# Extra matmuls of ones, an earlier first mask, and values weighed before scores in a twelve-sublayer decoder

## The chip, the core and the metric

The kernel runs on one core of one Trainium2 chip. The metric is the device time of one execution in microseconds (us). A core has five engines with instruction queues of their own: TensorE (PE in the profile; PEld is its weight load), VectorE (DVE), ScalarE (ACT), GpSimd (POOL) and SyncE (SP, which issues DMAs). Each takes its own instructions in order, and semaphores connect them.

## The reference

A batch of 16 sequences of 64 tokens with 128 features passes through four decoder layers. Each of the twelve sublayers is followed by a residual sum and a layer normalization. What is computed, cut to the calls:

```python
x = _layernorm(x + linear_attention(x))                 # 16 heads of 8
x = _layernorm(x + cross_attention(ctx, x, ctx, mask))  # xa0: 16 heads
x = _layernorm(x + local_block(x))                      # lb: two layers of local attention and a gated MLP
x = _layernorm(x + self_attention(x))                   # at1
x = _layernorm(x + cross_attention(x, ctx, ctx))        # xa1
x = _layernorm(x + sorted_ffn(x))                       # sf: only half 0 has work
x = _layernorm(x + recurrence(x))                       # rc: relu(mix), decaying scan, projection
x = _layernorm(x + cross_attention(x, ctx, ctx, mask))  # xa2: 32 heads
x = _layernorm(x + switch_ffn(x))                       # sw: 16 experts, top 1
x = _layernorm(x + relative_attention(x))               # at3
x = _layernorm(x + cross_attention(x, ctx, ctx, mask))  # xa3
x = _layernorm(x + top2_ffn(x))                         # tt: 8 experts, top 2
```

Linear attention normalizes queries and keys to unit length, forms `A = k^T (v * w)` for each token position over the batch, and gives `q A`. The local block normalizes queries and keys, turns them by position, and takes a softmax over the tokens of a window of 64, before and after which half of the features are shifted by one token.

## The kernel before

**Layout.** The 1024 tokens are two halves of 512 (8 sequences each). Activations lie token by token (`xt`, 128 tokens by 4 by 128 features) and flipped (`x`, features by 512 tokens). PSUM is shared out as two buffers of two banks for scores (pool `psc`, tag `sc`) and four buffers of one bank for everything else (pool `pt`, tag `t`). A tile waits until an earlier user of its buffer has been read.

**The order of the work.** The kernel is written as Python generators, one for each half; `side_by_side` takes a step of each in turn, with half 0 five steps ahead in the first stream (xa0, lb, at1, xa1, sf, rc, xa2). The framework's scheduler then sets the order in which each engine's queue holds the instructions, so an added instruction can move others. At sw both halves meet; a second stream (at3, xa3) and tt follow.

**`keep_busy`** (L153) issues one matmul of a bf16 tile of ones with itself, 512 columns wide. Its result is overwritten by the next real matmul into the same PSUM tile; it exists only to give TensorE something to do.

**Linear attention** (L266) works in four pairs of groups of 128 rows. `front` projects into `la_ps`, squares, and gets inverse roots (L764). `back` multiplies the three parts of `la_ps` by their factors (L314, DVE) into `la_four`, spreads values on POOL (L321, `la_sq`), multiplies keys by values (L327, `la_a`), masks on DVE (L329, `la_am`), transposes the queries (L333, into `la_o`), applies `la_am` (L339), and flips back (L346, L348, L351). `la_ps` and `la_o` share the four `t` buffers.

**Attention** (`attention`, L408): keys are copied under a mask for each head (L441, POOL, `km`), a unit of scores is made (L480) with its mask added by a matmul (L491), DVE takes maximum and difference (L536, L537), ACT the exponential (L540), `turn` transposes (L551, L554), `weigh` multiplies by the values (L572), and `gather` flips the result. Masks are made at their first use; xa0's `mask_outer` (L698) has two DMAs on SP (L704), a POOL multiply (L709, `mo_m`) and a DVE conversion to bf16 (L710, `mo_b`).

**The local block** (`local_half`, L784) runs its two units u through `rotate` (L807 to L840, `lb_qk`), `flip` (L862 to L869), `weights` (L880 to L905: scores `lb_sc`, maximum, difference, exponential), `turn` (L914), `weigh` (L932 to L949, `lb_av`, `lb_ao`), `gather` (L957, `lb_pao`) and `put` (L968), then the MLP (L1043 to L1063, `lb_pg`, `lb_pa`, `lb_pw`).

**The end of a sublayer** (`close`, L185): statistics on DVE (L195, L197), the inverse deviation on POOL (L201, L204, `rstd`), the normalized tokens on DVE (L206, `xt`), and then in `flip` an optional number `ones` of `keep_busy` matmuls, four transposes into `px` (L224, or L235 with the shift) and a copy by ACT (L226).

**The recurrence** (L1115) mixes neighbours on DVE (L1127, L1128), projects (`rc_p`, L1132), takes a ReLU on ACT (L1134), scans on DVE (L1137), and projects back (`po_rc`, L1142).

Of the kernel before, what the change touches and what calls it, by code (L numbers as in the profile page):

```python
# [37 lines left out]
class Kernel:  # L38
# [227 lines left out]
    def linear_attention(self):  # L266


        nc, work, psc, pt = self.nc, self.aw, self.psc, self.pt
        att = self.buf(4, [N], "la_att")  # L270
        att_b = att.rearrange("p (s b j) -> p s b j", b=S // 2, j=2)
        blk8 = self.g("blk8").unsqueeze(1).to_broadcast([P, 8, P])
        pos4 = self.g("pos4").unsqueeze(2).to_broadcast([P, 4, P])

        def front(pair):
            ss = work.tile([P, 2, 32], F32, tag="la_ss", name=f"la_ss{pair}")
            made = []
            for i in range(2):
                gr = pair * 2 + i
                ps = self.psum(pt, f"la_ps{gr}")  # L280

                for _ in range(12 if gr == 0 else 1):
                    self.keep_busy(ps)
                w = self.g("L0a_w")
                n = w.shape[1]
                nc.tensor.matmul(
                    ps[:, :n], self.x_all[:, bass.ts(gr, P)], w, start=True, stop=False
                )

                rows = [self.la_b] if pair == 0 else la_b3  # L290
                ones = self.g("one") if pair == 0 else self.ones_b
                for row in rows:
                    nc.tensor.matmul(
                        ps[:, :n], ones[0:1, :], row, start=False, stop=row is rows[-1]
                    )
                sq = self.buf(2, [HALF], f"la_sq{gr}")
                nc.scalar.activation(sq[:, 0:256], ps[:, 0:256], AF.Square)
                nc.vector.tensor_reduce(
                    ss[:, i, :], sq[:, 0:256].rearrange("p (n d) -> p n d", d=8), AX.X, ALU.add
                )  # L300
                gates = work.tile([P, 32], F32, tag="la_g", name=f"la_g{gr}", bufs=4)
                nc.scalar.activation(gates, ps[:, 384:416], AF.Sigmoid)
                made.append((ps, sq, gates))
            return made, self.inverse_root(work, ss.rearrange("p i n -> p (i n)"), f"la_{pair}")

        def back(pair, made, rs):
            for i, (ps, sq, gates) in enumerate(made):
                gr = pair * 2 + i
                four = self.buf(2, [4, P], f"la_four{gr}")
                rq = work.tile([P, 16], F32, tag="la_rq", name=f"la_rq{gr}")  # L310
                nc.vector.tensor_tensor(rq, rs[:, i * 32 : i * 32 + 16], gates[:, 16:32], ALU.mult)
                factors = (rq, rs[:, i * 32 + 16 : i * 32 + 32], gates[:, 0:16])
                for n, by in enumerate(factors):
                    nc.vector.tensor_tensor(  # L314
                        four[:, n, :].rearrange("p (h d) -> p h d", d=8),
                        ps[:, bass.ts(n, P)].rearrange("p (h d) -> p h d", d=8),
                        by.unsqueeze(2).to_broadcast([P, 16, 8]),
                        ALU.mult,
                    )
                vm = sq.rearrange("p (i d) -> p i d", d=P)  # L320
                nc.gpsimd.tensor_tensor(  # L321
                    vm, four[:, 2, :].unsqueeze(1).to_broadcast([P, 4, P]), pos4, ALU.mult
                )
                a = psc.tile([P, 2, HALF], F32, tag="sc", name=f"la_a{gr}")
                for t in range(2):
                    r = slice(64 * t, 64 * t + 64)
                    nc.tensor.matmul(a[:, t, :], four[r, 1, :], sq[r, :], start=True, stop=True)  # L327
                am = self.buf(4, [8, P], f"la_am{gr}")
                nc.vector.tensor_tensor(  # L329
                    am, a.rearrange("p t (i d) -> p (t i) d", d=P), blk8, ALU.mult  # L330
                )
                po = pt.tile([P, 4, P], F32, tag="t", name=f"la_o{gr}")
                nc.tensor.transpose(po[:, 0, :], four[:, 0, :], self.g("ident"))  # L333
                nc.scalar.copy(four[:, 3, :], po[:, 0, :])

                for m in range(2):
                    for j in range(4):
                        at = (m * 4 + j) // 2 * 32
                        nc.tensor.matmul(  # L339
                            po[32 * j : 32 * j + 32, 1 + m, :],  # L340
                            four[:, 3, at : at + 32],
                            am[:, m * 4 + j, :],
                            start=True,
                            stop=True,
                        )
                nc.scalar.copy(four[:, 0:2, :], po[:, 1:3, :])  # L346
                for m in range(2):
                    nc.tensor.transpose(po[:, 1 + m, :], four[:, m, :], self.g("ident"))  # L348
                to = po[:, 1:3, :].rearrange("p m (a b) -> p m a b", b=64)
                for j in range(2):  # L350
                    nc.scalar.copy(  # L351
                        att_b[:, :, gr * 4 : gr * 4 + 4, j].rearrange("p s (m a) -> p m a s", m=2),
                        to[:, :, :, 48 * j : 48 * j + 16],
                    )
        fronts = [front(0)]
        la_b3 = []
        rows3 = self.lbp.tile([P, 2080], F32, tag="v0", name="la_b3").bitcast(BF16)
        for i in range(3):
            row = rows3[0:1, bass.ts(i, 416)]
            nc.vector.tensor_copy(row, self.la_b)  # L360
            if i < 2:
                nc.vector.tensor_tensor(self.la_b, self.la_b, row, ALU.subtract)
            la_b3.append(row)
        for pair in range(4):
            if pair < 3:
                fronts.append(front(pair + 1))
            back(pair, *fronts[pair])
        return self.project_close(pt, self.g("L0a_wo"), att, "L0a_bo", "la")


# [37 lines left out]
    def attention(  # L408
        self, h, tag, kv, hd, scale, wq, wk, wv, wo, bq=None, bk=None, bv=None, bo=None,
# [4 lines left out]
        work, psc, pt = self.aw, self.psc, self.pt  # L414
# [104 lines left out]
        y = self.new_y(tag, h) if wo is None else None  # L519
# [101 lines left out]
        if wo is not None:  # L621
            for u in list(aos):
                gather(u)
            ps = pt.tile([P, 4, D], F32, tag="t", name=f"po_{tag}{h}")
            for i in range(4):
                self.group(ps[:, i, :], [(att[:, bass.ts(i, P)], self.g(wo))])
            y = self.new_y(tag, h)
# [6 lines left out]
            else:  # L634
                nc.vector.tensor_tensor(y, ps, base, ALU.add)

        ones = 8 if h == 1 and tag in ("xa2", "xa3") else 1
        flip = self.close(pt, h, y, tag, shift=tag == "xa0", ones=ones)
        yield "last"
        flip()  # L640
# [143 lines left out]
    def local_half(self, h):  # L784

        nc = self.nc
        work, psc, pt = self.aw, self.psc, self.pt
# [3 lines left out]
        for l in range(2):  # L791
            tag = f"lb{l}{h}"
# [195 lines left out]
            turn(0)  # L988
            flip(1)
            yield  # L990
            weights(1)
            weigh(0)
            yield
            turn(1)
            gather(0, 1)
# [24 lines left out]
            ps = self.psum(pt, f"{tag}_phn")  # L1020
# [31 lines left out]
            ps = pt.tile([P, 4, D], F32, tag="t", name=f"{tag}_pw2")  # L1052
# [8 lines left out]
            if l == 0:  # L1061
                x_in = self.buf(2, [4, D], f"{tag}_x2")
                nc.vector.tensor_tensor(x_in, ps, base, ALU.add)  # L1063
                self.shifted(self.psum(pt, f"{tag}_px"), h, x_in)
                yield
            else:
                y = self.new_y("lb", h)
                nc.vector.tensor_tensor(y, ps, base, ALU.add)
                flip = self.close(pt, h, y, "lb")
                yield "last"  # L1070
                flip()

# [2 lines left out]
    def sorted_ffn(self, h):  # L1075
        nc, pt = self.nc, self.pt
        yield
        x = self.x[h]
        if h == 1:
            flip = self.close(pt, h, self.xt[h], "sf")  # L1080
# [10 lines left out]
        for c in range(8):  # L1091
            if c % 4 == 0:
                hids.append(self.buf(8, [4, HALF], f"sf_hid{c}"))
            ps = self.psum(pt, f"sf_p{c}")
# [10 lines left out]
        y = self.new_y("sf", h)  # L1105
        for i in range(4):
            nc.vector.scalar_tensor_tensor(
                y[:, i, :], acc[:, i, :], ws[:, i : i + 1], self.xt[h][:, i, :], ALU.mult, ALU.add
            )
        flip = self.close(pt, h, y, "sf")  # L1110
        yield "last"
        flip()

# [1 line left out]
    def recurrence(self, h):  # L1115
        nc, pt, sc = self.nc, self.pt, self.scalars
# [12 lines left out]
            inp[:, :, 1:S], x3[:, :, 0 : S - 1], rest, inp[:, :, 1:S], ALU.mult, ALU.add  # L1129
        )  # L1130
        ps = self.psum(pt, f"rc_p{h}")
        self.group(ps, [(self.g("rc_win"), inp.rearrange("p b s -> p (b s)"))])  # L1132
        hid = self.buf(2, [HALF], f"rc_hid{h}")
        nc.scalar.activation(hid, ps, AF.Relu, bias=self.g("rc_bin"))  # L1134
# [3 lines left out]
            st, dec.rearrange("p b s -> p (b s)"), hid, 0.0, ALU.mult, ALU.add  # L1138
        )
        ps = pt.tile([P, 4, D], F32, tag="t", name=f"po_rc{h}")  # L1140
        for i in range(4):
            self.group(ps[:, i, :], [(st[:, bass.ts(i, P)], self.g("rc_wout"))])  # L1142
        y = self.new_y("rc", h)
        nc.vector.tensor_tensor(y, ps, base, ALU.add)
        flip = self.close(pt, h, y, "rc")
        yield "last"
        flip()

# [863 lines left out]
```

## Time and profile before

| what | us |
|---|---|
| median of 3 runs | 896.4 (886.66 to 896.52) |
| the profiled execution | 871.75 |
| its span, first to last instruction | 869.8 |
| TensorE busy | 717.0 (82%) |
| VectorE busy | 481.7 (55%) |
| ScalarE busy | 354.9 (41%) |
| GpSimd busy | 254.0 (29%) |
| mean granted TensorE clock | 0.893 of full speed |

The profile is one execution. Busy time is time in which an engine had an instruction running. PEclk is the clock that TensorE was granted, in tenths of full speed. A row of the timeline gives start, duration, engine, source line, operation, the tiles written and read, shapes and a count, and in brackets how long the engine was idle before it and which instruction ended that. An f32 matmul leaves two records for each instruction, so "x8" is four matmuls.

### The profile page before, as it was taken

To read this page: it belongs to the slowest core of one execution; us is meant where nothing else is said; L and a number is where in the kernel's file an instruction comes from. 1 tells how busy PE (TensorE), PEld (TensorE's weight loads), DVE (VectorE), ACT (ScalarE), POOL (GpSimd) and SP (SyncE) were. 2 spreads that over 40 slices of the span, in tenths; PEclk is the share of its full clock that TensorE was granted. 3 is DMA by queue.
4 is the path that set the end of the run, shared out by engine and by line. 5 is a ranking of instruction groups with operands and counts; after the bars stand their busy time and mean duration, and the time that the engine had idled before them with its cause. 6 is when DMAs were issued, how large, how long until landed. Compare 5 with 4: busy or idle time off the path is not lost.

```text
span 869.8 us, 17379 instructions
## 1 busy us (share of the span) xinstructions
PE 717.0 (82%) x7045; PEld 455.8 (52%) x7045; DVE 481.7 (55%) x1103; ACT 354.9 (41%) x584; POOL 254.0 (29%) x289
## 2 busy tenths in 40 slices
PE   6777979878888699789996999977947999967990
PEld 2333646555545466546573557644633565744770
DVE  4556466574665745447525766544542565656563
ACT  2223547445454444445551445522304554522330
POOL 2314135070432703130305220016151111025732
PEclk7878989889999998989996989988977799978995
DMA  7900000000000000140000000051115625031102
GB/s 277 273 1 25 2 1 2 14 1 2 1 2 1 1 2 2 40 155 2 2 2 0 1 2 2 2 151 48 50 41 148 198 54 184 2 122 37 53 25 83
DMA packets 34504, 43.65 MB, mean 50 GB/s; under 512 B 7524, under 2 KB 26469, under 8 KB 33784
## 3 DMA queue, kind: packets, MB, share of 16 engines
q1 hardware_dynamic: 32344, 38.26, 14.1%
q0 software_dynamic: 2080, 4.26, 1.7%
q8 instruction: 58, 0.95, 0.5%
q14 instruction: 22, 0.18, 0.1%
HBM read 34.31 MB, written 11.61 MB: 53 GB/s over the span
## 4 chain that ended last, share of the span: by engine, by line
PE 51%; DVE 18%; POOL 9%; issue 6%; ACT 4%; DMA 4%; SPq 1%; DVEq 0%; POOLq 0%; ACTq 0%
PE xa_sc L480 5%; PE xa_av L572 4%; PE xa_pt L551 3%; PE sw_pe L151 2%; PE at_sc L480 2%; PE lb_qk L151 2%; DVE lb_t L818 2%; PE at_av L572 2%; PE xa_sc L491 2%; DMA at_mem<-at_rsb 2%; DVE lb_t L832 2%; PE xa_pt L156 2%; PE at_pt L551 1%; PE lb_pf L868 1%; PE lb_pw L151 1%
## 5 line engine op out<-in xcount | busy, mean ns | idle before, releaser
L536 DVE TENSOR_REDUCE xa_mx<-xa_sc 128x16 f32<-128x1024 f32 x40 | 48.7, 1218 | 63.8 <-PE xa_sc L491 41.4
L838 POOL TENSOR_TENSOR lb_t<-lb_t,lb_t 128x1024 f32<-128x1024 f32 x16 | 37.7, 2357 | 99.4 <-DVE lb_t L832 95.2
L554 ACT COPY xa_eT<-xa_pt 128x512 f32<-128x512 f32 x80 | 45.5, 587 | 40.8 <-PE xa_pt L551 40.0
L540 ACT ACTIVATE xa_e<-xa_e 128x1024 f32<-128x1024 f32 x40 | 42.3, 1058 | 37.2 <-DVE xa_e L537 37.1
L480 PE MATMUL xa_sc<-xa_km,xa_q 32*64 32x256 f32 x640 | 55.2, 404 | 0.7 <-ACT xa_q L431 0.5
L551 PE MATMUL xa_pt<-const,xa_e 128*128 128x128 f32 x320 | 48.8, 280 | 1.8 <-ACT xa_e L540 1.8
L441 POOL TENSOR_SCALAR xa_km<-xa_k,const 128x512 f32<-128x512 f32 x40 | 27.1, 695 | 79.3 <-ACT xa_k L429 46.0
L537 DVE TENSOR_TENSOR xa_e<-xa_sc,xa_mx 128x1024 f32<-128x1024 f32 x40 | 48.7, 1217 | 2.1
L551 PEld LDWEIGHTS xa_pt<-const,xa_e 128*128 128x128 f32 x320 | 40.3, 145 | 13.1 <-ACT xa_e L540 3.7
L572 PEld LDWEIGHTS xa_av<-v,xa_eT 128*64 128x64 f32 x1280 | 40.5, 138 | 8.2 <-issue 6.1
L572 PE MATMUL xa_av<-v,xa_eT 128*64 128x18 f32 (+1 forms) x1280 | 44.2, 209 | 0.0
L156 PEld LDWEIGHTS <-ones_b 128*128 128x128 bf16 x255 | 24.8, 104 | 36.4 <-issue 19.9
L151 PE MATMUL lb_qk<-w,lb_hs 128*128 128x512 f32 x64 | 35.8, 686 | 8.5 <-DVE lb_t L832 4.8
L480 PEld LDWEIGHTS xa_sc<-xa_km,xa_q 32*64 32x64 f32 x640 | 24.7, 136 | 19.9 <-issue 12.8
L814 DVE TENSOR_REDUCE lb_ss<-lb_t 128x16 f32<-128x1024 f32 x16 | 19.5, 1217 | 27.9 <-ACT lb_t L811 27.9
L201 POOL TENSOR_TENSOR rstd_xa<-mv_xa,eps 128x4 f32<-128x4 f32 x8 | 1.6, 201 | 112.2 <-DVE mv_xa L197 112.2
L156 PE MATMUL xa_pt<-ones_b 128*128 128x512 bf16 x80 | 30.2, 390 | 0.0
L862 POOL TENSOR_TENSOR lb_t<-lb_t,lb_rs 128x1024 f32<-128x1024 f32 x16 | 30.1, 1904 | 0.0
L868 PE MATMUL lb_pf<-const,lb_t 128*128 128x128 f32 x128 | 20.1, 312 | 9.4 <-POOL lb_t L862 9.3
L480 PE MATMUL at_sc<-at_km,at_q 32*64 32x256 f32 x256 | 22.5, 452 | 5.2 <-DVE at_rel L533 3.7
L533 DVE TENSOR_TENSOR at_rel<-at_rel,at_sc 128x1024 f32<-128x1024 f32 x8 | 9.7, 1212 | 29.2 <-DMA at_mem<-at_rsb 16.4
L554 ACT COPY at_eT<-at_pt 128x512 f32<-128x512 f32 x32 | 17.6, 586 | 19.3 <-PE at_pt L551 13.4
(474 smaller groups left out, 1715.0 us busy)
## 6 DMA issues: line engine op xcount, KB each, us to landing
sw_gu<-in_sw_gu SPq DMA_DIRECT2D x4, 1024.0 KB, 8.3
at_mem<-at_rsb SPq DMA_DIRECT2D x16, 256.0 KB, 2.9
at_rel<-at_mem SPq DMA_DIRECT2D x32, 128.0 KB, 3.0
w<-in_w SPq DMA_DIRECT2D x1, 3114.0 KB, 12.2
sw_dn<-in_sw_dn SPq DMA_DIRECT2D x4, 512.0 KB, 7.0
tt_w<-in_tt_w SPq DMA_DIRECT2D x2, 1024.0 KB, 8.6
tt_b<-in_tt_b SPq DMA_DIRECT2D x1, 2048.0 KB, 7.1
sw_in<-in_zeros SPq DMA_DIRECT2D x1, 1472.0 KB, 11.6
```

Source lines behind the costliest of these rows:

```text
L151: self.nc.tensor.matmul(out, lhsT, rhs, start=n == 0, stop=n == len(pairs) - 1)
L156: self.nc.tensor.matmul(out, self.ones_b, self.ones_b.unsqueeze(1).to_broadcast([P, 4, P]), start=True, stop=True)
L480: nc.tensor.matmul(sc[64 * j : 64 * j + 64, gg, at : at + 256], q[r, t], part[r, :, t] if local else part[r, :, :], start=not masked or (p ...
L536: nc.vector.tensor_reduce(mx, scored, AX.X, ALU.max)
L537: nc.vector.tensor_tensor(e3, scored, mx.unsqueeze(2).to_broadcast([P, 16, S]), ALU.subtract)
L540: nc.scalar.activation(e3, e3, AF.Exp, scale=scale)
L551: nc.tensor.transpose(ps[:, bass.ts(n, P)], blocks[:, bass.ts(n, P)], self.g("ident"))
L554: nc.scalar.copy(eT[:, gg, :], ps)
L572: nc.tensor.matmul(av[64 * j : 64 * j + 64, pr, hp, :, :], eT[:, gg, at : at + 64], v[:, b, hp, :, :], start=True, stop=True,)
L838: nc.gpsimd.tensor_tensor(t1, t1, t2.rearrange("p t n d -> p t (n d)"), ALU.add)
L862: nc.gpsimd.tensor_tensor(t3, t3, rs[:, bass.ts(r, 16)].unsqueeze(2).to_broadcast([P, 16, 64]), ALU.mult)
L868: nc.tensor.transpose(ps[:, c, :], t1[:, t, bass.ts(c, P)], ident)
```

## The change

The change has three parts. First, it adds `keep_busy` matmuls: in `back` of linear attention ahead of the query transpose (ten for the first group of the first pair, four for the first group of the other pairs, two for the second group of each pair), in the recurrence ahead of both projections (six in half 0, three in half 1), and in the `flip` at the end of xa0 in half 0 (four instead of one), of the local block (two in half 0, seven in half 1, none before), of the sorted layer in half 0 and of the recurrence (four instead of none). Second, xa0's mask is made at the end of linear attention's loop instead of inside xa0. Third, in the local block `weigh(0)` is called ahead of `weights(1)`.

```diff
@@ linear_attention, back
                 po = pt.tile([P, 4, P], F32, tag="t", name=f"la_o{gr}")
+
+                for _ in range((10 if pair == 0 else 4) if i == 0 else 2):
+                    self.keep_busy(po.rearrange("p n m -> p (n m)"))
                 nc.tensor.transpose(po[:, 0, :], four[:, 0, :], self.g("ident"))
@@ linear_attention, end
             back(pair, *fronts[pair])
+
+        self.masks["xa0"] = self.mask_outer(work)
         return self.project_close(pt, self.g("L0a_wo"), att, "L0a_bo", "la")
@@ attention
-        ones = 8 if h == 1 and tag in ("xa2", "xa3") else 1
+        ones = 8 if h == 1 and tag in ("xa2", "xa3") else 4 if h == 0 and tag == "xa0" else 1
@@ local_half
+            weigh(0)
             weights(1)
-            weigh(0)
@@ local_half, end
-                flip = self.close(pt, h, y, "lb")
+                flip = self.close(pt, h, y, "lb", ones=2 + 5 * h)
@@ sorted_ffn
-        flip = self.close(pt, h, y, "sf")
+        flip = self.close(pt, h, y, "sf", ones=4)
@@ recurrence
         ps = self.psum(pt, f"rc_p{h}")
+        for _ in range(6 - 3 * h):
+            self.keep_busy(ps)
         self.group(ps, [(self.g("rc_win"), inp.rearrange("p b s -> p (b s)"))])
...
         ps = pt.tile([P, 4, D], F32, tag="t", name=f"po_rc{h}")
+        for _ in range(6 - 3 * h):
+            self.keep_busy(ps.rearrange("p i d -> p (i d)"))
...
-        flip = self.close(pt, h, y, "rc")
+        flip = self.close(pt, h, y, "rc", ones=4)
```

The lines named in this text are those of the kernel before.

## The prediction

> **What bounds the kernel now.** I read the page first, then the TensorE clock in stretches, then the timeline where the clock or a wait stood out.
>
> ```profile
> span 869.8 us, 17379 instructions
> PE 717.0 (82%) x7045; PEld 455.8 (52%) x7045; DVE 481.7 (55%) x1103; ACT 354.9 (41%) x584; POOL 254.0 (29%) x289
> PEclk7878989889999998989996989988977799978995
> PE 51%; DVE 18%; POOL 9%; issue 6%; ACT 4%; DMA 4%; SPq 1%; DVEq 0%; POOLq 0%; ACTq 0%
> ```
>
> TensorE is half of the chain that ended last, and it seldom has its whole clock. The clock changes on a grid of 3.41 us; cut on that grid (us, PE busy with records, clock, DMA):
>
> ```profile
> 31.87:35.28 3.41, 1.43 (x7) 1.00 1.02 231
> 35.28:38.70 3.42, 3.42 (x8) 0.50 0.91 215
> 76.24:79.66 3.42, 0.99 (x10) 1.00 0.01 2
> 79.66:83.07 3.41, 3.41 (x24) 0.50 0.02 5
> 366.37:369.79 3.42, 0.21 (x8) 1.00 0.81 264
> 369.79:373.20 3.41, 2.32 (x7) 0.50 0.96 332
> ```
>
> A thin step is followed by one at half clock. Over the span before 790 us: of 16 full-clock steps under 0.45 busy, 15 were followed by half clock; from 0.45 to 0.6, 5 of 12; from 0.6 to 0.75, 5 of 20; above that, none of 135. About 167 us before 851 us run at half clock. So a stall is paid twice: as itself, then in the matmuls behind it. A matmul of ones (`keep_busy`) takes 0.215 us at full clock (four from 98.85 to 99.71) and 0.43 at half (470.47 to 470.90), so one fills 6% of a step.
>
> Here a **rule** speaks against the change. The Trainium skill, "TensorE: Matmul & The Clock Gate", Part 1: The HAM clock gate, has the clock fall after a whole idle window of about 3.4 us, and puts the ramp's penalty under 1% of a typical span. By that, thin steps would keep their clock, all clock gains here would stay under 8.7 us, and ones in thin steps would only cost. The rows say otherwise: 1.43 us of work in 3.41 did not keep it. I take the rows; the sum by the rule is the second rival.
>
> These rows carry the rest:
>
> ```profile
> 20.00 0.45 PE L333 MATMUL la_o<-const,la_four 128*128 128x128 f32 x1 [4.03 <-DVE la_root L781]
> 78.67 0.59 PE L491 MATMUL xa_sc<-mo_b,ident_b 128*128 128x512 bf16 x2 [3.40 <-DVE mo_b L710]
> 114.72 6.61 PE L151 MATMUL lb_qk<-w,lb_hs 128*128 128x512 f32 x8 [2.48 <-ACT lb_hs L238]
> 210.00 0.94 PE L957 MATMUL lb_pao<-const,lb_ao 128*128 128x128 f32 x4 [1.90 <-DVE lb_rc L942]
> 370.20 0.47 PE L224 MATMUL px_lb<-const,xt_lb 128*128 128x128 f32 x1 [3.62 <-DVE xt_lb L206]
> 460.97 2.04 PE L151 MATMUL rc_p<-rc_inp,w 128*128 128x512 f32 x2 [2.34 <-issue]
> 471.63 4.70 POOL L441 TENSOR_SCALAR xa_km<-xa_k,const 128x512 f32<-128x512 f32 x7
> 471.68 2.73 DVE L206 TENSOR_SCALAR xt_rc<-y_rc,mv_rc,rstd_rc 128x128 f32<-128x128 f32 x4 [2.26 <-POOL rstd_rc L204]
> ```
>
> Each bracket is the engine's idle time before the row and its releaser.
>
> **The parts.** The change adds 72 ones: 30 in linear attention, 3 at the first cross attention, 9 at the local blocks' end, 30 in the sorted layer and the recurrence. At full clock that is 15.5 us of TensorE; what counts is where they stand.
>
> **Mask, gain 5.3.** The mask's DMAs now wait only for a buffer that `la_a` of group 4 frees near 49 us; with issue 1.3 and landing 3.5 they are in by 54. POOL's multiply (1.04) stands behind the last `la_sq`, done at 56.3; DVE's conversion (0.43) goes between the last two `la_am`, costing at most 0.4 there. On SP they pass the load of w7, which waits for the output projection anyway. So scores begin without the 3.40 us stall. What is late next is DVE: maximum and subtraction are 2.4 us a unit, first at 75.8 behind `xt_la` instead of 79.30. At full clock (scores 1.1 instead of 1.58 and 1.98, transposes 1.1 instead of 1.64) the fourth unit's maximum comes at 85.8 where it came at 91.13. If half clock stays, 3.4 is left.
>
> **Linear attention, loss 1.1.** The ten ones of pair 0 seem to fit the 4.03 us idle, but they write `la_o`, whose PSUM buffer `la_ps` holds until the third L314 row ends at 19.85; that, not the square root, released L333 at 20.00. So they stand *behind* the wait: 10 x 0.43 = 4.3 us, then transpose, two ones, transpose, and `la_a` starts near 25.5 instead of 22.17. Full clock arrives at 25.04 in both, so eight records take 1.8 instead of 3.39: `la_am` slips from 24.30 to 26.5, 2.1 us lost. Bounds: nothing, if the clock rises at 21.6, and 4.3, if it doesn't rise at 25. Pairs 1 and 2: three ones fit the idle before `la_a` (0.85), but DVE, busy with roots until 38.07, holds the next step, so warm matmuls gain nothing; two ones ahead of L348 cost 0.2 to 0.3. Pair 3: DVE waits 3.73 for `la_a`, where full clock brings 1.5. Sum -2.1 - 0.5 + 1.5; range -4 to +2.
>
> **First cross attention, 0.** Two of its four ones stand before the `xa_pt` transposes, two behind. The thin stretch runs from 109.73 to 114.72 with 1.1 us of work; 0.43 more leaves under 0.45 of a step. `lb_qk` stays at half clock. If it didn't, 1.6.
>
> **Values in front of scores, gain 4.5.** In a local block `lb_av` followed `lb_sc`, and the `lb_pao` transposes stalled for 1.90 us while DVE did a 1.2 us maximum and a subtraction first. Now `lb_av` starts at 205.3, DVE's first two reciprocals and multiplications end at 207.3 behind the last `lb_hid`, `lb_pao` runs to 208.15, `lb_sc` fills what was stall, and `lb_pw` starts at 209.6 instead of 210.78. The block's own exponential comes 2.4 us later, but its `lb_pt` waited behind `lb_pw` and `lb_px` anyway, until 215.5. So 1.15 for each of three such places and 1.0 for the first; range 2 to 6.
>
> **Local block's end, gain 1.7.** Half 1: seven ones and two moved ones (2.0 us) fill the 3.62 us idle, and its step goes from 0.06 busy to about 0.6. If the clock holds, `at_pq` and `at_pk` take 1.0 each instead of 2.07 and 1.91. Between 0 and 2.3. Half 0: two ones in 0.59 idle, nothing.
>
> **Sorted layer and recurrence, gain 3.5.** Half 0: between `px_sf` and `rc_p` stand ten records' worth of work: two ones of `rc_p`, sixteen `xa_av`, six ones of `po_rc`: 2.6 us against 2.34 idle, and DVE takes a reciprocal first, so `rc_p` starts 0.6 later. At full clock it and `po_rc` take 1.0 each instead of 2.04 and 2.08, so statistics come 1.5 us earlier. Then POOL: the new order puts `rstd_rc` behind seven `xa_km` (7 x 0.67 from 464.6, when `xa_k` comes), so it ends at 471.2 instead of 471.64. But POOL is then quiet, so four `xt_rc` take 1.1 (as beside quiet POOL at 457.13), not 2.73. TensorE meanwhile idles about 3.5 us, longer than px_rc's four ones and sixteen `xa_pv` cover, so I expect half clock again there. Scores start near 477.2 instead of 479.6, and half 1's `px_xa` 4 us sooner. Half 1: its ten ones lie among half 0's scores; they cost up to 2 and may save the half clock of 502.9 to 509.7. Range 0 to 6.
>
> **Sum:** 5.3 - 1.1 + 0 + 4.5 + 1.7 + 3.5 = 13.9 us. All of it lies before the switch layer's start at 581 us, which needs both halves; the stretches between, at 384 to 456 and 510 to 575, keep TensorE full, and a shift passes through them. The profiled execution took 871.75 us (span 869.8 and 1.95 around it), so 857.9 there. The runs' median is 896.4, 24.6 above it with no reason in the profile; I carry the difference: **882.4 us**. No change is known from these runs within 2%, 18 us.
>
> **Rivals.** (1) *The clock holds nearly everywhere.* The stretches beside the edits (48.9 to 59.2, 79.7 to 86.5, 113.8 to 120.6, 154.8 to 158.2, 369.8 to 376.6, 458.5 to 468.8, 472.2 to 479, 502.9 to 509.7) make 58 us; half of that by TensorE's 51% of the chain is 15 us, where I counted 6.6: 874. For it: the sharp edge near half busy. Against: ones stand in front of transposes, and stalls behind these stay. (2) *The clock doesn't follow the ones* (the rule): mask 3.4 and values 4.5, less pair 0's 2.1 and 0.5: 5.3, so 891. (3) *Ones stand on the path.* They start only when a buffer comes free, as at pair 0, and matmuls run in order. If all do, 72 x 0.215 is 15.5 and pair 0's half clock 2.6 more, 18.1 against 7.9 gained: 10.2 slower, 906.6. From 37 ones on the path it cancels. Against: at 370, 458 and 461 the wait is a DVE or POOL chain that starts when the ones' buffer is already free.
>
> **Chances:** forecast 0.46, (1) 0.28, (2) 0.18, (3) 0.08. Runs before spread over 10 us, so of the forecast 0.3 falls under 878.5, of (1) 0.85: faster 0.38. Of (3) 0.4 and of (2) 0.1 may pass 914: slower 0.05. The range 864 to 898 leaves out the low end of (1) and most of (3).
>
> **What would show it.** Right: no wait of L491 on `mo_b`; full clock from 76 to 90; `la_am` of pair 0 two us later; the `lb_pao` stall near 1 us; half clock still at the first `lb_qk`; `rstd_rc` behind `xa_km`. Wrong: half clock after 367 or at `rc_p` as before, or `la_am` not late.

## The result, and the profile after

The changed kernel took 883.38 us (median, 875.69 to 892.43), the one before 889.33 in the same set of runs (884.20 to 896.52): ratio 0.9917, 95% interval 0.9888 to 0.9947. A second set gave 869.91 against 876.30, ratio 0.9918 (0.9895 to 0.9942). That is 7.3 us faster, with about 5 to 10 us as the interval, where 13.9 were forecast. That the forecast time of 882.4 came close is luck: the median of before, 896.4 over three runs, fell to 889.3 over twenty. The ratios, here and below, leave out slow runs (over 1.5% above the fastest of the same kernel), the medians keep them.

The page after:

```profile
span 879.4 us, 17518 instructions
PE 736.0 (84%) x7115; PEld 465.1 (53%) x7117; DVE 480.5 (55%) x1103; ACT 354.6 (40%) x584; POOL 254.0 (29%) x289
PEclk8899989989999899999996999969877999957996
PE 50%; DVE 17%; POOL 9%; issue 6%; ACT 5%; DMA 4%; SPq 1%; another core or an unknown queue 1%; DVEq 0%; POOLq 0%; ACTq 0%
```

TensorE is 19 us busier. Over the span it has no more clock: 184.2 us at half clock, 186.0 before. Ahead of the switch layer's logits, where the change lies, half clock did fall (in the stages A to F below from 93.9 us to 83.9 and, profiled a second time, 81.0); behind them, where the code is the same, it rose from 83.6 to 98.4 and 100.7. The profiled execution of before (871.75 us) was one of its fastest, so spans of the two profiles cannot be subtracted: from the logits to the end of the span it took 288.4 us, and the changed kernel 303.1 and, the second time, 295.2. I compare stages ahead of that point. Steps of the changed kernel on the clock's grid, thin ones and those behind them (us, PE busy with records, clock, DMA share, GB/s):

```profile
70.64:74.06 3.42, 2.48 (x30) 1.00 0.00 0
74.06:77.47 3.41, 3.41 (x14) 0.50 0.00 0
77.47:80.88 3.41, 3.41 (x39) 1.00 0.02 5
108.19:111.60 3.41, 1.10 (x4) 1.00 0.01 2
111.60:115.02 3.42, 2.42 (x3) 0.50 0.00 0
364.19:367.60 3.41, 1.75 (x6) 1.00 0.92 310
367.60:371.02 3.42, 3.42 (x22) 0.50 1.05 398
463.17:466.59 3.42, 1.10 (x5) 1.00 0.00 0
466.59:470.00 3.41, 3.10 (x6) 0.50 0.00 0
483.65:487.07 3.42, 3.42 (x8) 0.50 0.00 0
487.07:490.48 3.41, 3.41 (x51) 1.00 0.03 5
```

Of the thin steps that the change aimed at, two with 1.10 us of work each are left: ahead of the first `lb_qk` and in the recurrence's wait. Behind the second, half clock lasts 20.5 us, from 466.59 to 487.07. The rows of the timeline that answer to those shown before (source lines in rows of a changed kernel are that kernel's own, a few higher than those of the kernel before):

```profile
17.98 4.42 PE L156 MATMUL la_o<-ones_b 128*128 128x512 bf16 x10 [4.28 <-DVE la_root L786]
22.20 0.42 PE L336 MATMUL la_o<-const,la_four 128*128 128x128 f32 x1
78.63 0.60 PE L496 MATMUL xa_sc<-mo_b,ident_b 128*128 128x512 bf16 x2
112.60 6.58 PE L151 MATMUL lb_qk<-w,lb_hs 128*128 128x512 f32 x8 [2.48 <-ACT lb_hs L238]
204.22 0.68 PE L962 MATMUL lb_pao<-const,lb_ao 128*128 128x128 f32 x4
365.17 1.09 PE L224 MATMUL px_lb<-const,xt_lb 128*128 128x128 f32 x4 [1.57 <-DVE xt_lb L206]
454.81 1.02 PE L151 MATMUL rc_p<-rc_inp,w 128*128 128x512 f32 x2
457.79 4.91 POOL L446 TENSOR_SCALAR xa_km<-xa_k,const 128x512 f32<-128x512 f32 x7 [2.13 <-ACT xa_k L436]
463.49 1.02 POOL L204 TENSOR_TENSOR rstd_rc<-rstd_rc,minus 128x4 f32<-128x4 f32 x1
464.55 1.12 DVE L206 TENSOR_SCALAR xt_rc<-y_rc,mv_rc,rstd_rc 128x128 f32<-128x128 f32 x4 [2.30 <-POOL rstd_rc L204]
464.95 0.58 PE L224 MATMUL px_rc<-const,xt_rc 128*128 128x128 f32 x2 [2.77 <-DVE xt_rc L206]
```

The waits for `mo_b` and of `lb_pao` are gone, `rc_p` runs at full clock in 1.02 us, and pair 0's ten ones stand behind their wait for 4.42 us, ahead of the transpose. Then `px_rc` waits, by way of `xt_rc`, for POOL, whose `rstd_rc` came behind seven `xa_km`.

Where the time went, by stage (us, one profiled execution each, worked out from the traces; but for the start of A, from the ends of tiles). A: from the start of the fourth `la_four` of linear attention's pair 0 (L314) to half 1's `xt_la`; B: to half 0's `xt_xa` of the first cross attention; C: to half 0's first `lb_x`; D: to half 1's `y_lb`; E: to the first `x_at`; F: to half 1's logits of the switch layer. A begins at the start column, which depends on loads and clock ahead of the change.

| kernel | start | A | B | C | D | E | F |
|---|---|---|---|---|---|---|---|
| before | 19.9 | 55.9 | 36.0 | 102.6 | 151.8 | 16.4 | 198.7 |
| after | 17.9 | 59.8 | 32.0 | 100.3 | 151.2 | 14.9 | 200.2 |
| after, again | 17.4 | 60.2 | 32.0 | 100.3 | 151.3 | 14.9 | 200.2 |
| mask alone | 19.9 | 55.9 | 30.5 | 101.5 | 151.5 | 16.4 | 199.1 |
| values alone | 20.0 | 55.9 | 41.2 | 99.2 | 150.8 | 16.2 | 198.6 |
| ones alone | 17.4 | 59.8 | 43.3 | 101.4 | 151.6 | 14.4 | 194.2 |
| mask, values | 18.5 | 55.9 | 30.5 | 98.8 | 150.8 | 16.4 | 202.1 |
| mask, values, local end | 17.2 | 54.8 | 30.5 | 99.6 | 149.0 | 14.4 | 198.4 |
| no linear-attention ones | 18.2 | 55.9 | 30.5 | 99.4 | 150.7 | 14.8 | 200.3 |
| filled | 17.5 | 58.6 | 32.0 | 99.9 | 152.8 | 14.4 | 195.6 |
| filled, no linear-att. ones | 17.0 | 57.4 | 30.5 | 99.6 | 146.8 | 14.7 | 197.0 |
| filled, fewer | 16.4 | 54.0 | 32.0 | 97.9 | 150.1 | 15.0 | 196.0 |
| filled, fewer, again | 19.0 | 57.8 | 32.0 | 100.1 | 150.7 | 14.9 | 193.8 |

A single execution of a stage moves by a few us with where half clock falls, so I trust a difference where several rows agree.

### The profile page after: what moved, and what is told of

Its sections match the earlier page's. It is cut to its first block, busy times and chain, and to the rows that moved or that the text cites. A ratio compares the mean times of both kernels' runs of the same rounds, so it can differ in the third digit from the quotient of the medians.

```text
span 879.4 us, 17518 instructions
## 1 busy us (share of the span) xinstructions
PE 736.0 (84%) x7115; PEld 465.1 (53%) x7117; DVE 480.5 (55%) x1103; ACT 354.6 (40%) x584; POOL 254.0 (29%) x289
## 4 chain that ended last, share of the span: by engine, by line
PE 50%; DVE 17%; POOL 9%; issue 6%; ACT 5%; DMA 4%; SPq 1%; another core or an unknown queue 1%; DVEq 0%; POOLq 0%; ACTq 0%
PE xa_sc L485 5%; PE xa_av L577 4%; PE xa_pt L556 3%; PE sw_pe L151 2%; PE lb_pf L873 2%; PE xa_sc L496 2%; POOL lb_t L867 1%; PE xa_pt L156 1%; PE at_pt L556 1%; PE lb_po L151 1%; PE at_av L577 1%; DVE lb_t L837 1%; DVE lb_t L823 1%; DVE xa_e L542 1%; PE lb_qk L151 1%
## 5 line engine op out<-in xcount | busy, mean ns | idle before, releaser
L843 POOL TENSOR_TENSOR lb_t<-lb_t,lb_t 128x1024 f32<-128x1024 f32 x16 | 37.7, 2356 | 98.8 <-DVE lb_t L837 94.6
L156 PEld LDWEIGHTS <-ones_b 128*128 128x128 bf16 x327 | 32.3, 106 | 54.2 <-issue 35.1
L485 PE MATMUL xa_sc<-xa_km,xa_q 32*64 32x256 f32 x640 | 54.8, 407 | 1.5 <-DVE xa_e L542 0.9
L446 POOL TENSOR_SCALAR xa_km<-xa_k,const 128x512 f32<-128x512 f32 x40 | 27.3, 699 | 85.2 <-ACT xa_k L434 46.3
L485 PEld LDWEIGHTS xa_sc<-xa_km,xa_q 32*64 32x64 f32 x640 | 24.6, 137 | 21.6 <-issue 16.2
L873 PE MATMUL lb_pf<-const,lb_t 128*128 128x128 f32 x128 | 22.3, 337 | 10.3 <-POOL lb_t L867 10.2
L873 PEld LDWEIGHTS lb_pf<-const,lb_t 128*128 128x128 f32 x128 | 19.4, 177 | 12.7 <-POOL lb_t L867 11.7
L538 DVE TENSOR_TENSOR at_rel<-at_rel,at_sc 128x1024 f32<-128x1024 f32 x8 | 9.6, 1212 | 29.2 <-DMA at_mem<-at_rsb 14.6
L1345 POOL DMA_INDIRECT tt_got<-tt_in,tt_ids x20 | 19.2, 959 | 19.8 <-DVE tt_ids L1322 6.7
```

Source lines behind the costliest of these rows:

```text
L156: self.nc.tensor.matmul(out, self.ones_b, self.ones_b.unsqueeze(1).to_broadcast([P, 4, P]), start=True, stop=True)
L485: nc.tensor.matmul(sc[64 * j : 64 * j + 64, gg, at : at + 256], q[r, t], part[r, :, t] if local else part[r, :, :], start=not masked or (p ...
L843: nc.gpsimd.tensor_tensor(t1, t1, t2.rearrange("p t n d -> p t (n d)"), ALU.add)
L873: nc.tensor.transpose(ps[:, c, :], t1[:, t, bass.ts(c, P)], ident)
```

## The experiments

The theory: half clock follows thin steps, ones help where they fill a thin step and cost where they stand on the path. Its rivals: the clock holds nearly everywhere (1), doesn't follow the ones (2), or the ones stand on the path (3).

### The change in three parts

**Mask alone.** (added to the kernel before)

```diff
+        self.masks["xa0"] = self.mask_outer(work)
         return self.project_close(pt, self.g("L0a_wo"), att, "L0a_bo", "la")
```

> The first mask alone, made within linear attention; no ones added, scores ahead of values as before. Forecast: 5.3 us faster, ratio 0.994: no wait of the first masked scores on mo_b, full clock from 76 to 90 us, and the fourth unit's maximum near 86 instead of 91. If the clock does not come with it: 3.4 us, 0.996, with half clock still somewhere from 79 to 87. If what linear attention lost in the changed kernel (la_am of pair 3 2.2 us later than before) is the mask's doing, because its conversion stands between la_am 6 and 7 on DVE, then la_am ends near 63 here as well and the net is about 2 us; if the ones did it, la_am of pair 3 ends near 61.5.

885.24 against 888.74, ratio 0.9955 (0.9928 to 0.9982): 4.0 us. B is 30.5 instead of 36.0, with full clock from 59 to 107 us, the fourth unit's maximum comes at 85.6 (forecast 85.8), and linear attention is untouched: A is 55.9, and its last `la_am` ends at 61.1 as before. So the mask is worth about what was forecast, and what linear attention lost is not its doing.

**Values ahead of scores, alone.** (on the kernel before)

```diff
+            weigh(0)
             weights(1)
-            weigh(0)
```

> Values in front of scores in the local blocks alone. Forecast: 4.5 us faster, 1.1 a place, ratio 0.995, with the lb_pao stall near 1 us instead of 1.90. If the block's exponential, which now comes 2.4 us later, becomes the late one instead, nothing: 1.000, and lb_pt waits for lb_e. If it costs a thin step and so a half clock behind the projection: up to 3 us slower, 1.003.

884.38 against 888.74, ratio 0.9924 (0.9888 to 0.9960): 6.8 us. With the mask this pair is 0.9959 of the mask alone (0.9914 by 0.9955), 3.6 us. The traces give 3.4 (C from 102.6 to 99.2) and 1.0 (D). B is 41.2 here with the same code as before: there the half clock behind the mask's stall lasted 20.4 us instead of 6.8.

**Ones alone.**

```diff
-        self.masks["xa0"] = self.mask_outer(work)
...
-            weigh(0)
             weights(1)
+            weigh(0)
```

(taken from the changed kernel)

> All 72 ones, without the mask's move and without the swap. Forecast: 4.1 us faster (linear attention -1.1, local block's end +1.7, sorted layer and recurrence +3.5), ratio 0.995. Rival 1 (the clock holds nearly everywhere): the same less the stretch at the mask, some 8 us faster, 0.991. Rival 2 (the clock doesn't follow the ones): 2.6 slower, 1.003, with as much half clock as before. Rival 3 (ones stand on the path): 18 slower less what little clock they save, 1.01 to 1.02.

888.14 against 888.74, ratio 0.9962 (0.9930 to 0.9993): 3.4 us by the ratio, within 0.6 and 6.2, and 0.6 by the medians. The profiled execution was one of this kernel's longer ones (span 892.3), and I rely only on what others repeat: A is 59.8 as in the changed kernel, E is 14.4. It has the recurrence's thin step too, with a short half clock behind it, and F is 194.2; for this no second execution of the kernel was taken:

```profile
472.84:476.26 3.42, 1.05 (x27) 1.00 0.02 5
476.26:479.67 3.41, 2.29 (x6) 0.50 0.00 0
479.67:483.08 3.41, 3.41 (x15) 0.50 0.00 0
483.08:486.50 3.42, 3.42 (x42) 1.00 0.01 2
```

**Mask and values, no ones.** The change without its five `ones=` edits and three `keep_busy` loops.

> Mask and values as changed, without the 72 ones. Forecast: 9.8 us faster, ratio 0.989, so slower than the changed kernel by 4.1. Rival 1: slower than the changed kernel by 8 or more. Rival 2: 7.9 faster, 0.991, and faster than the changed kernel by 2.6. Rival 3: faster than the changed kernel by 10 or more, near 0.982.

879.67 against 888.74, ratio 0.9914 (0.9889 to 0.9939): 7.6 us. The whole change has 0.9917 and 0.9918. So, **beside the mask and the values, the 72 ones together are worth nothing**, within about 3 us, where 4.1 were forecast. What follows asks where their gain went.

### Which ones cost, and which thin steps are left

These four ran in one set, beside a before of 887.85 us.

**Without linear attention's ones.**

```diff
-                for _ in range((10 if pair == 0 else 4) if i == 0 else 2):
-                    self.keep_busy(po.rearrange("p n m -> p (n m)"))
```

> The changed kernel without the thirty ones of linear attention. If they stand on the path there (from pair 0's la_am to pair 3's, 36.5 us in the changed kernel against 34.3 in the one before and in the one with the mask alone): 2 us faster than the changed kernel, ratio to before near 0.9895, and that distance is 34.3 again. If they buy clock that is used later: as slow as the changed kernel or slower, 0.992 to 0.994.

875.24, ratio 0.9858 (0.9803 to 0.9912), 0.6% ahead of the changed kernel, but measured in another set and with overlapping intervals. The stage decides: A is 55.9 again, against 59.8 and 60.2 with them, although this execution's half clock began at 16.3 us, as good as the changed kernel's 16.0. They stand on the path, and cost 4 us, not 1.1. In these traces they save no half clock either: within A it is 18.8 us before, 18.6 and 19.1 in the changed kernel, and 18.6 here; of the four traces with them, only the filled kernel's has less, 10.0.

**Mask, values and the local blocks' end.**

```diff
-                flip = self.close(pt, h, y, "lb")
+                flip = self.close(pt, h, y, "lb", ones=2 + 5 * h)
```

(on the kernel with mask and values)

> Mask and values, and of the ones only those at the local blocks' end (two and seven). If these are worth the 1.7 us that was forecast, from y_lb of half 1 to the first x_at is 14.5 us instead of 16.3, and the ratio to before near 0.9895 (0.9914 without them). If the sorted layer's and the recurrence's ones were worth 3.5 us more, the changed kernel stays ahead of this one; if these give back what they gain, this one is 2 us ahead of the changed kernel.

876.26, ratio 0.9882 (0.9830 to 0.9933). E is 14.4 instead of 16.4; it is 14.4 to 15.0 in all nine traces that have these ones, and 16.2 to 16.4 in the other four. The 1.7 us forecast are there. In the three traces where no half clock followed (this one, the ones alone, the filled one) E is 14.4; in the other six 3.4 us of half clock followed, and it is 14.7 to 15.0. Against the changed kernel the ratio alone doesn't tell.

**The two thin steps filled.** (on the changed kernel)

```diff
+                    for _ in range(10 if l == 0 and h == 0 and c == 0 else 0):
+                        self.keep_busy(qk[:, 0, :])
...
-        flip = self.close(pt, h, y, "rc", ones=4)
+        flip = self.close(pt, h, y, "rc", ones=16 - 12 * h)
```

> The changed kernel with ones in the two thin steps that it keeps: ten in front of the first lb_qk, behind the px_xa transposes, and sixteen instead of four in front of half 0's px_rc. By the rows (a full-clock step under 0.45 busy is followed by half clock) these two steps go to 0.7 or more: no half clock from 111 to 118 us (3.3 us) and none of the 20.5 us from 466.6 (5 to 10 us): 8 to 12 us faster than the changed kernel, 0.978 to 0.983 of before. If the clock doesn't follow ones: as the changed kernel, 0.992, with the same half clock. If they stand on the path: 26 x 0.215 or up to 5 us slower, 0.997.

877.23, ratio 0.9877 (0.9820 to 0.9934): less than forecast, and too wide an interval to tell it from the changed kernel's 0.9917. The clock held in this execution. The same two places on the grid:

```profile
109.42:112.83 3.41, 1.87 (x6) 1.00 0.00 0
112.83:116.25 3.42, 3.42 (x21) 1.00 0.03 5
460.99:464.40 3.41, 1.62 (x9) 1.00 0.00 0
464.40:467.82 3.42, 3.42 (x40) 1.00 0.02 5
```

The steps came to 0.55 and 0.47 busy, not 0.7 as expected, and neither is followed by half clock: there is none from 75 to 126 us and none between 335 and 566. The three filled kernels that follow agree at `lb_qk` (3.70 us in all four); at the recurrence's wait their steps were 0.47, 0.60 and 0.48 busy and were followed by 3.4 us of half clock each, not by 20.5. So the ones are shown to shorten half clock there, and to avoid it in one execution of four; rival 2 falls with this all the same. The timeline of the first filled kernel shows what it is worth (its view begins at 460 us and so counts eleven of the sixteen ones):

```profile
110.98 3.70 PE L151 MATMUL lb_qk<-w,lb_hs 128*128 128x512 f32 x8 [1.54 <-ACT lb_hs L238]
459.78 2.54 PE L156 MATMUL px_rc<-ones_b 128*128 128x512 bf16 x11
464.10 1.10 PE L224 MATMUL px_rc<-const,xt_rc 128*128 128x128 f32 x4 [1.79 <-DVE xt_rc L206]
```

`lb_qk` takes 3.70 us instead of 6.58, yet `lb_x` comes only 0.4 sooner behind it (C 99.9 instead of 100.3). A further step, at 126.5 to 129.9 us, has lost its clock by then; whether that is the whole reason is not shown. The ones of `px_rc` lie inside the wait, and F falls from 200.2 to 195.6.

**Filled, with fewer ones.** As the last, without linear attention's ones and without half 1's ten of the recurrence (the first line changes nothing, since half 1 of the sorted layer closes on another line, without ones):

```diff
-        flip = self.close(pt, h, y, "sf", ones=4)
+        flip = self.close(pt, h, y, "sf", ones=4 - 4 * h)
...
-        for _ in range(6 - 3 * h):
+        for _ in range(6 - 6 * h):
...
-        flip = self.close(pt, h, y, "rc", ones=16 - 12 * h)
+        flip = self.close(pt, h, y, "rc", ones=16 - 16 * h)
```

> As the run before, but without the ones of linear attention and without half 1's ones in the sorted layer and the recurrence, which stand among half 0's scores. If those only cost: 2 us (linear attention) and up to 2 (half 1) faster than the run before, 0.974 to 0.980 of before. If half 1's ones save the half clock behind its recurrence: no faster than the run before, with half clock near 495 to 505.

867.38, ratio 0.9769 (0.9705 to 0.9832): faster than both kernels, and its interval lies clear of the changed kernel's.

### The same three again

Three more in one set, beside a before of 876.30 us: the changed kernel itself, the last version again, and the filled one without linear attention's ones but with half 1's.

> The changed kernel itself again, beside the two that follow, so that the three are compared within one set of runs. 0.989 to 0.995 of before. Its profile is a second execution of the same program: if the place and the length of half clock are set by the program, the stretch behind the recurrence is 20 us again; if they are chance, one of the short ones, 3.4 to 10 us, as in the runs with the same thin step there (6.8 with the ones alone).

869.91, ratio 0.9918. Its trace repeats the first one's clock:

```profile
463.14:466.55 3.41, 1.10 (x5) 1.00 0.00 0
466.55:469.96 3.41, 3.07 (x6) 0.50 0.00 0
483.62:487.03 3.41, 3.41 (x8) 0.50 0.00 0
487.03:490.44 3.41, 3.41 (x51) 1.00 0.02 5
```

The 20 us are no chance of one execution; the kernel without linear attention's ones has them too (460.0 to 480.5).

> The version with the two thin steps filled, without the ones of linear attention and of half 1's sorted layer and recurrence, again, beside the changed kernel: if its 0.977 was no luck, 9 us or more ahead of the changed kernel (0.990 of it or less).

861.58, ratio 0.9822 (0.9772 to 0.9871), 8.3 us below the changed kernel's median beside it, where 9 or more were expected; against before, 15.6 us. The first set's 0.977 lies at the lucky end, the lead is no luck.

> The two thin steps filled, without the ones of linear attention alone; half 1's ones in the sorted layer and the recurrence stay. If linear attention's ones were the whole cost: as fast as the version without both (0.977 of before). If half 1's ones cost too, up to 2 us behind it, 0.979. If linear attention's ones cost nothing, as with them: 0.988.

861.14, ratio 0.9856 (0.9807 to 0.9905). The medians of the two versions are 0.4 us apart, their ratios 0.3%, with overlapping intervals: linear attention's ones are the cost that shows; whether half 1's ones cost up to 2 us stays open.

## Why the prediction was right and where not

- **Mask, 5.3.** Right: 5.5 in B and 4.0 by the ratio, alone. In the changed kernel B gains 4.0: half clock lies at 74.06 to 77.47, across the queries' projection. So the forecast full clock "from 76 to 90" begins 1.5 us late.
- **Linear attention, -1.1: the step that failed first.** Measured, -3.9, at the very end of its range of -4 to +2. Pair 0 was right: from the fourth L314 to the end of `la_am` 8.9 us instead of 6.9, the forecast 2.1. That `la_am` nevertheless ends at 26.8 in both traces is because the changed kernel's execution reached L314 2.0 us sooner, ahead of the change; the forecast sign "`la_am` two us later" must be read from L314. Pairs 1 and 2 lost 0.5 each (14.1 to 14.6, 12.6 to 13.1), twice the 0.5 in all. Pair 3 was to gain 1.5 and lost 1.2 (7.6 to 8.8 from `la_am` to `la_am`). Of its rows after:

```profile
57.56 1.12 PE L327 MATMUL la_a<-la_sq,la_four 64*128 64x512 f32 x2
58.62 0.61 PE L156 MATMUL la_o<-ones_b 128*128 128x512 bf16 x2
58.73 1.22 DVE L329 TENSOR_TENSOR la_am<-la_a,const 128x1024 f32<-128x1024 f32 x1 [3.23 <-PE la_a L327]
59.06 0.27 PE L336 MATMUL la_o<-const,la_four 128*128 128x128 f32 x1
60.89 1.12 PE L327 MATMUL la_a<-la_sq,la_four 64*128 64x512 f32 x2
62.05 1.23 DVE L329 TENSOR_TENSOR la_am<-la_a,const 128x1024 f32<-128x1024 f32 x1 [1.77 <-PE la_a L327]
```

  and before:

```profile
56.51 3.29 PE L327 MATMUL la_a<-la_sq,la_four 64*128 64x512 f32 x8
58.63 2.44 DVE L329 TENSOR_TENSOR la_am<-la_a,const 128x1024 f32<-128x1024 f32 x2 [3.73 <-PE la_a L327]
```

  The full clock came as forecast, but with the ones the order that TensorE is given changed around them. A `la_a` consists of matmuls on the upper and the lower 64 rows; where they follow each other directly, their records begin together and lie side by side: eight in 3.29 us above, at half clock, or in 1.99 at full clock, at pair 0 of the changed kernel:

```profile
23.27 1.99 PE L327 MATMUL la_a<-la_sq,la_four 64*128 64x512 f32 x8
```

  In pair 3 of the changed kernel other matmuls and ones stand between the two, and the records come one after the other: four times 1.12 us, 4.48 in all, at full clock. That is so in all four traces with linear attention's ones and in none of the nine without; two of these nine (local end; filled, fewer) have full clock at pair 3 as well, and there the eight records take 1.99 us. The second group's `la_a` stands behind the first group's. So DVE's second `la_am` starts at 62.05, where the two had run in direct succession from 58.63 to 61.07. The prediction had priced the clock of these matmuls and not their order.
- **First cross attention, 0.** Right: `lb_qk` 6.58, half clock as before.
- **Values ahead of scores, 4.5.** Mechanism right, size 2.9 in the changed kernel (2.3 in C, 0.6 in D), 3.6 and 6.8 by the ratios of the two pairs. At the three first places `lb_pw` starts 3.7 us behind the last `lb_pa` instead of 5.4, so 1.7 each, more than the 1.0 and 1.15 forecast; at the last 0.2. But from `lb_pw` to the next `lb_pa` the three stretches between take 1.0, 1.6 and 0.4 longer. One cause can be seen in the second. With the swap, the step ahead of the next block's second `lb_pf` can be thin enough to cost the clock; rows of the kernel with mask and values:

```profile
235.01:238.42 3.41, 1.40 (x10) 1.00 0.00 0
238.42:241.83 3.41, 3.41 (x18) 0.50 0.00 0
```

  and of the one with the mask alone:

```profile
240.13:243.54 3.41, 1.97 (x15) 1.00 0.00 0
243.54:246.95 3.41, 3.41 (x20) 1.00 0.00 0
```

  The sixteen `lb_pf` take 3.31 us in the first and 1.97 in the second. Both have the same 1.66 us wait for the exponential ahead of it; where the grid cuts the stall differs. In all three traces without the swap these `lb_pf` take 1.97 us; in the ten with it 1.97 once and 2.3 to 3.3 nine times. So this goes with the swap, but how much it costs depends on the grid.
- **Local block's end, 1.7.** Right: 1.5 (E), 2.0 where the clock held. The step rose to 0.51 busy, not 0.6, and was followed by half clock all the same, but for 3.4 us instead of 6.8.
- **Sorted layer and recurrence, 3.5: the step that failed second.** No gain is measured: F is 200.2 to 200.3 in the three traces that have these ones beside mask and values, and 198.4 to 202.1 in the five without any of them. Its first half holds: `rc_p` and `po_rc` at 1.02 and 1.16 us, `rstd_rc` behind the `xa_km`, `xt_rc` in 1.12 us, half 0's `x_rc` 13.9 us behind its `x_sf` instead of 16.6. The failure is the sentence "so I expect half clock again there", which was left without a price: `px_rc` waits 2.77 us, the step is 0.32 busy, and the clock stays at half for 20.5 us. Before, the same wait was shorter, its step was 0.49 busy, and 6.8 us of half clock followed:

```profile
468.77:472.19 3.42, 1.69 (x11) 1.00 0.00 0
472.55 0.44 PE L224 MATMUL px_rc<-const,xt_rc 128*128 128x128 f32 x1 [1.56 <-DVE xt_rc L206]
```

  Half 1's `x_rc` comes 23.8 us behind its `x_sf` instead of 17.2. Over the whole of F, half clock is 27.3 us before and 24.4 after: what the ones saved at `rc_p` came back behind `px_rc`. Filling that wait gives F of 193.8 to 197.0 in the four traces of the filled kernels. Why this spell lasted six steps, and only two in the kernel with the ones alone behind a step as thin, stays open.

The measured stages, A to F, sum to a gain of 3.0 us (4.0 - 3.9 + 2.9 + 1.5 - 1.5) where the ratio says 7.3; each falls short of its forecast, by 1.3, 2.8, 1.6, 0.2 and 5.0. The traces are each one position of the clock's grid, the runs average over many; I could not bring the two closer. One time in the prediction is misread: 0.43 us for a matmul of ones at half clock is right, but stands at 472.79 to 473.22, and at 470.47 there is none.

Of the rivals, (2), the rule of the Trainium skill in "TensorE: Matmul & The Clock Gate", Part 1, that the clock falls after a whole idle window, falls as the condition for losing it: over the thirteen traces up to 785 us, 148 of 150 full-clock steps under 0.45 busy were followed by half clock, 76 of 176 from 0.45 to 0.6, 49 of 252 from 0.6 to 0.75, and 23 of 1805 above (busy shares rounded to hundredths); and filling two of the steps took half clock away or shortened it. The 1% that the prediction takes from the same part is said there of the ramp at a kernel's start; it gave no bound of 8.7 us here, where half clock fills 186.0 of 869.8 us. (1) fell short: in the stages A to F half clock fell by 10 to 13 us only, of the 58 that it counted on. (3) is right for thirty of the 72 ones, and for these alone shown.

## What to carry to other kernels

Work that only keeps a clock up pays where the engine would wait for something that is already on its way. It costs where its own buffer is what the engine waits for (2 us at pair 0), and where it pushes apart matmuls that would have run side by side (1.2 us at pair 3). Of the 72 ones here, 30 cost 4 us; with these and half 1's ten gone, and 22 more in the two waits left, the kernel gained 8. Price a remaining thin step by the longest half clock that such a step has shown, not by the shortest. And compare the parts of a change by what each is worth beside the others: mask, values and ones gave 4.0, 6.8 and 3.4 us alone by their ratios, and 7.3 together.

## What was not expected of the hardware

In these traces, two matmuls on different 64 rows run beside each other only where nothing stands between them: eight records of `la_a` take 1.99 us in the one case and 4.48 in the other, both at full clock. An edit that brings other matmuls between them can cost more than the time of what it adds.

Half clock comes in whole steps of 3.41 us: of those that begin before 850 us and end before the program does, the thirteen traces show 132 spells of one step, 105 of two, 45 of three, 16 of four, and then 5 of six and 8 of seven, none of five. In the one from 466.59 to 487.07 TensorE was busy for 3.10 us of the first step and throughout the last, so a busy step alone doesn't end them; what does is open.

Where the grid lay alike, a program repeated itself: both traces of the changed kernel have their first half clock at 16.0 us and the same spells to 0.1 us in nearly all places up to 630 us. Where it lay otherwise, the same program differed: the two executions of the filled version with fewer ones began half clock at 15.4 and 10.9 us and took 54.0 and 57.8 us for stage A. That the grid's position is the cause of the spread from run to run fits this, but was not tested.
